# Four-layer graph network on one Trainium2 core: three steps of the next layer's projection change places beside the second attention

## The chip, the cores and the metric

The kernel runs on one core of one Trainium2 chip. The metric is the device time of one execution in microseconds. Three timed runs of the kernel before gave 2900.37, 2915.1 and 2917.88 us; the median is 2915.1. Beside them one execution was profiled, and it took 2553.76 us itself.

## The reference

There are 3327 nodes with 512 features each and a sparse 0/1 adjacency matrix. Four layers follow each other, each with a residual and a normalization ahead of it:

```
h = relu(layernorm(x));  x = x + layer(h, adj)
layer 0, 2, 3 (graph attention, 8 heads of 64):
    Wh = h @ W                       per head
    e[i,j] = leaky_relu(f_dst[i] + f_src[j], 0.2), only where adj[i,j] > 0
    out[i] = softmax_j(e[i,j]) @ Wh  (then a batch norm and relu, or an elu)
layer 1 (sage): relu(concat(h @ Ws, mean_of_neighbours(h) @ Wn) @ Wc)
```

The part that matters here is the step from layer 2 to layer 3. Layer 3 needs, for every node, its projected row Wh and two score terms per head. They can be made for a block of 128 nodes as soon as layer 2 has finished that block.

## The kernel before, in words

The nodes are cut into 26 blocks of 128, and each block into two groups of 64. For every group a list of neighbours is built first; the lists are up to 22 chunks of 128 neighbours long at the beginning and get shorter to 5 and 4 chunks at the end (`CAPS`). The attention, `attend`, walks over all groups in order. Its inner loop runs over units of at most three chunks:

- GpSimd (POOL) gathers the rows of the unit's neighbours out of a table in DRAM (L1165). A row holds 8 x 65 values scaled by exp(score) and 8 further factors.
- VectorE (DVE) takes the maximum of the row's factors and of the group's own factors R (L1266, `mx`), and multiplies by the mask (L1273, `wgt`). R comes from a small DRAM array, is loaded as `r_two`, and is spread over all partitions by a matmul (L1198, `r_bc`).
- TensorE multiplies weights and rows into `facc` (L1287).

Within the attention the order of instructions on TensorE, VectorE and ScalarE (ACT) is the order in which the Python code issues them, and every engine works its instructions off in that order. After each unit's two VectorE instructions, and before its matmuls, the loop calls `later()`. This advances each group that is being finished by one step (`sums`, `rd`, the eight scalings `fhp`, then `fin_e` and `fin_x`, which write the block of x), and then calls `tick()` of the next layer's projection.

That projection is the class `Following`. A finished block first goes through the normalization (`norm`, L777, in three steps: `ln_j`, `rs_h` and its companions, `ln_h`). Then a generator, `rest` (L841), does the block in steps that end at a `yield`. A tick advances the oldest block by one step, or by two where a second block is waiting; when a block ends, the next one begins in the same step:

```
for _ in range(min(2, len(self.ready))):
    while self.ready and next(self.ready[0]) is None:
        self.ready.pop(0)
```

The steps of `rest` before are: transposes into `p_ps` and relus into `hT` (L845, L848); scores `p_sd`, two exps into the row, and the copy `s_col` (L853 to L860); the clamp of `s_col` on VectorE and the matmuls `p_wh` (L863, L866); the two ACT instructions of `halves` that make `r_full` and `r_half` (L730, L731), the eight scalings `v_row` (L870) and the store of the table's rows; the subtraction that makes the lower half of R on VectorE (L734) and the transpose `p_tr` (L874); the copy `r_row` and its store to DRAM (L877 to L882). The PSUM tiles `p_ps`, `p_sd`, `p_wh` and `p_tr` of this layer share one buffer. Layer 2's own projection, beside layer 1, uses `rest_by_rows`, and layer 0's uses `Projection`; both call `halves` too.

When the last unit of layer 2 is done, `proj.drain()` runs the remaining ticks, and the last layer's attention begins.

Of the kernel before, what the change touches and what calls it, by code (L numbers as in the profile page):

```python
# [32 lines left out]
ALU = mybir.AluOpType  # L33
# [28 lines left out]
SMALL = 53.0  # L62
# [662 lines left out]
def halves(nc, pool, cs, sf):  # L725


    rf = pool.tile([P, H], F32, name="r_full", tag="r_full", bufs=2)
    rs = pool.tile([P, 2, H], F32, name="r_half", tag="r_half", bufs=2)
    nc.scalar.activation(rf, sf, AF.Exp, scale=0.8, bias=cs["down"])  # L730
    nc.scalar.copy(rs.bitcast(F32R)[:, 0, :], rf)  # L731

    def other():
        nc.vector.tensor_tensor(rs.bitcast(F32R)[:, 1, :], rf, rs[:, 0, :], ALU.subtract)  # L734
        return rs.rearrange("p t h -> p (t h)")

    return other


class Following:  # L740
# [100 lines left out]
    def rest(self, c, hx):  # L841
        nc, pp, WA, wl = self.tc.nc, self.pool, self.WA, self.wl
        tp = self.psum.tile([P, KC, P], F32, name="p_ps", tag="p_ps", bufs=self.pb)
        for kc in range(KC):
            nc.tensor.transpose(tp[:, kc, :], hx[:, kc * P : (kc + 1) * P], self.cs["ident"])  # L845
        hT = pp.tile([P, KC, P], F32, name="hT", tag="hT", bufs=2)
        for kc in range(KC):
            nc.scalar.activation(hT[:, kc, :], tp[:, kc, :], AF.Relu, accum_out=self.hs[:, c, kc : kc + 1])  # L848
        yield True
        self.mean(c, hT)  # L850
        sd = self.psum.tile([P, BANK], F32, name="p_sd", tag="p_ps", bufs=self.pb)
        for kc in range(KC):
            nc.tensor.matmul(sd[:, : 2 * H], hT[:, kc, :], WA[wl][:, kc, :], start=(kc == 0), stop=(kc == KC - 1))  # L853
        row = pp.tile([P, ROW], F32, name="v_row", tag="v_row", bufs=2)
        V = row[:, : H * (F + 1)].rearrange("p (h f) -> p h f", f=F + 1)
        d = sd[:, H : 2 * H]
        nc.scalar.activation(V[:, :, F : F + 1], d.rearrange("p (h o) -> p h o", o=1), AF.Exp)
        nc.scalar.activation(row[:, H * (F + 1) :], d, AF.Exp, scale=-0.8, bias=self.cs["down"])
        sf = pp.tile([P, H], F32, name="s_col", tag="s_col", bufs=2)
        nc.scalar.copy(sf, sd[:, :H])  # L860
        yield True

        nc.vector.tensor_scalar(sf, sf, -SMALL, SMALL, ALU.max, ALU.min)  # L863
        wh = self.psum.tile([P, D], F32, name="p_wh", tag="p_ps", bufs=self.pb)
        for kc in range(KC):
            nc.tensor.matmul(wh, hT[:, kc, :], self.Wt[:, kc, :], start=(kc == 0), stop=(kc == KC - 1))  # L866
        yield True
        rs = halves(nc, pp, self.cs, sf)
        for h in range(H):
            nc.scalar.mul(V[:, h, 0:F], wh[:, h * F : (h + 1) * F], V[:, h, F : F + 1])  # L870
        nc.sync.dma_start(self.table[c * P : (c + 1) * P, :ROW], row.bitcast(I32))
        yield True
        tr = self.psum.tile([2 * H, P], F32, name="p_tr", tag="p_ps", bufs=self.pb)
        nc.tensor.transpose(tr, rs(), self.cs["ident"])  # L874
        yield True
        rr = pp.tile([2 * H, P], F32, name="r_row", tag="r_row", bufs=2)
        nc.scalar.copy(rr, tr)  # L877
        n = P // GB
        nc.sync.dma_start(
            self.r_dram[c * n : (c + 1) * n, :, :, :].rearrange("g t h i -> (t h) g i"),  # L880
            rr.rearrange("h (g i) -> h g i", i=GB),
        )  # L882
        yield None
# [739 lines left out]
```

## Time and profile before

| | us |
|---|---|
| timed runs, median (lowest to highest) | 2915.1 (2900.37 to 2917.88) |
| profiled execution, its own time | 2553.76 |
| its span from the first to the last instruction | 2551.8 |
| DVE busy in the span | 1852.3 (73%) |
| PE busy in the span | 1825.0 (72%) |
| POOL busy in the span | 1387.4 (54%) |
| ACT busy in the span | 1068.3 (42%) |

The timed runs are 361 us longer than the profiled execution. The trace is of the profiled execution alone, so every duration below is compared with its 2553.76 us.

Lines such as "L870 ACT v_row" name the line of the kernel, the engine and the tile that is written. In timelines the first number is the start in microseconds from the beginning of the span, the second is the duration, and what stands in square brackets is the idle time of the engine just before and what ended it. "x8" counts instructions; a matmul of 32-bit numbers stands as two. In lists of waits the numbers are the total, the count and the longest, in microseconds. The stage of the change, in which layer 2's attention and layer 3's projection run side by side, lies between about 1500 and 2046 us of the span.

### The profile page before, as it was taken

The numbers are of one execution on the slowest core, as the hardware profiler recorded it, in microseconds if no ns is written. First come the engines' busy times: TensorE is split into PE (matmuls) and PEld (weight loads), VectorE is DVE, ScalarE is ACT, GpSimd is POOL, SyncE is SP. The second block draws the span as 40 slices with busy tenths as digits, with TensorE's granted clock in tenths as the row PEclk, the third lists the DMA queues.
The fourth block names the chain that finished last, engine by engine and source line by source line (L and its number), as shares of the span: only waits on it lengthen the run. The fifth ranks groups of instructions, "written<-read, shape, count | busy, mean of one in ns | idle before, by whom it ended". The sixth has DMA issues, their size and how long they took to land.

```text
span 2551.8 us, 53690 instructions
## 1 busy us (share of the span) xinstructions
PE 1825.0 (72%) x21112; PEld 1161.8 (46%) x21112; DVE 1852.3 (73%) x2272; ACT 1068.3 (42%) x3810; POOL 1387.4 (54%) x1482
## 2 busy tenths in 40 slices
PE   3667756776677698889999657778878646566653
PEld 2444444454454342223333356656555435555543
DVE  7667579999997850222333499999877279999996
ACT  4553212333445332334455214667766601233444
POOL 1000176777772026777777277776554067777672
PEclk9767889988888899999999778897877787777787
DMA  8773198888783566788888478887665178888784
GB/s 326 288 263 123 43 296 276 280 281 260 241 253 95 191 217 198 234 247 260 254 267 255 125 223 242 235 240 232 199 200 177 39 215 232 236 238 243 232 238 123
DMA packets 189057, 562.57 MB, mean 220 GB/s; under 512 B 37764, under 2 KB 42304, under 8 KB 185470
## 3 DMA queue, kind: packets, MB, share of 16 engines
q0 software_dynamic: 115456, 404.86, 53.3%
q1 hardware_dynamic: 73342, 154.20, 17.0%
q8 instruction: 169, 2.77, 0.4%
q14 instruction: 90, 0.74, 0.1%
HBM read 499.26 MB, written 59.68 MB: 219 GB/s over the span
## 4 chain that ended last, share of the span: by engine, by line
PE 30%; DVE 24%; issue 13%; ACT 9%; DMA 8%; POOL 3%; DVEq 0%; SPq 0%; POOLq 0%; ACTq 0%
DVE mx L1266 12%; PE facc L1287 8%; DVE wgt L1273 8%; PE sage_acc L1522 4%; DMA z_rows<-h_dram,idx 4%; PE p_wh L866 4%; DMA rows<-table,idx 3%; PE n_ps L1471 3%; PE p_wh L808 3%; ACT fhp L1225 2%; POOL z_rows L1165 2%; PE s_ps L1445 2%; POOL rows L1165 1%; ACT bn_y L1225 1%; ACT v_row L870 1%
## 5 line engine op out<-in xcount | busy, mean ns | idle before, releaser
L1165 POOL DMA_INDIRECT rows<-table,idx x1077 | 1027.7, 954 | 580.0 <-issue 224.5
L1287 PE MATMUL facc<-rows,wgt 128*64 128x65 f32 x17232 | 722.5, 253 | 393.7 <-DVE wgt L1273 259.7
L1287 PEld LDWEIGHTS facc<-rows,wgt 128*64 128x64 f32 x17232 | 667.1, 165 | 518.2 <-DVE wgt L1273 310.5
L1266 DVE TENSOR_TENSOR mx<-r_bc,rows 128x1536 f32<-128x1536 f32 (+1 forms) x405 | 639.4, 1579 | 48.4 <-DMA fin_x<-fx 17.7
L1273 DVE TENSOR_TENSOR wgt<-mx,mask 128x1536 f32<-128x1536 f32 (+1 forms) x405 | 638.4, 1576 | 42.3 <-DVE mx L1266 1.0
L1165 POOL DMA_INDIRECT z_rows<-h_dram,idx x359 | 340.7, 949 | 273.7 <-ACT hT L1442 141.0
L1225 ACT ACTIVATE fhp<-sums,rd 64x64 f32<-64x64 f32 x832 | 219.9, 334 | 305.4 <-DVE rd L1219 302.0
L1522 PE MATMUL sage_acc<-z_rows,z_mask 128*64 128x512 f32 x718 | 209.8, 618 | 33.0 <-DMA z_rows<-h_dram,idx 32.6
L1258 ACT ACTIVATE mask<-on 128x192 uint8<-128x192 uint16 (+1 forms) x135 | 46.5, 345 | 325.3 <-DVE on L1252 321.8
L1086 POOL DMA_DIRECT2D list_b<-shift x12 | 6.0, 503 | 271.7 <-DVE shift L1040 271.5
L811 DVE TENSOR_TENSOR sd_pr<-p_wh,ab 128x1024 f32<-128x1024 f32 x26 | 31.8, 1225 | 141.4 <-PE p_wh L808 141.4
L1522 PEld LDWEIGHTS sage_acc<-z_rows,z_mask 128*64 128x64 f32 x718 | 52.2, 137 | 156.2 <-issue 77.6
L680 PE MATMUL wh_ps<-fWt,hT 128*128 128x512 f32 x208 | 123.3, 748 | 0.0
L866 PE MATMUL p_wh<-fWt,hT 128*128 128x512 f32 x208 | 117.2, 714 | 1.4 <-ACT s_col L860 1.4
L1225 ACT ACTIVATE bn_y<-sums,rd 64x64 f32<-64x64 f32 x416 | 109.5, 333 | 2.4 <-DVE rd L1219 0.5
L1503 ACT CAST z_mask<-mask 128x128 f32<-128x128 uint8 (+1 forms) x196 | 52.7, 284 | 118.7 <-PE sage_acc L1522 117.5
L1476 DVE TENSOR_TENSOR s_o<-n_ps,bn_y 128x512 f32<-128x512 f32 x26 | 17.9, 690 | 116.2 <-PE n_ps L1471 116.2
L1215 ACT COPY sums<-facc 128x260 f32<-128x260 f32 x156 | 56.6, 363 | 104.7 <-DMA rows<-table,idx 77.7
L1471 PE MATMUL n_ps<-fWx,aT 128*128 128x512 f32 x208 | 98.7, 608 | 0.0
L808 PE MATMUL p_wh<-fWt,hT 128*128 128x512 f32 x208 | 96.9, 610 | 2.0 <-DVE hT L699 1.9
L1445 PE MATMUL s_ps<-fWx,hT 128*128 128x512 f32 x208 | 93.5, 603 | 3.4 <-ACT hT L1442 3.4
L1198 PE MATMUL r_bc<-r_two,fones 2*128 2x512 f32 x156 | 89.1, 575 | 6.6 <-DMA r_two<-r_dram 3.6
(213 smaller groups left out, 2146.3 us busy)
## 6 DMA issues: line engine op xcount, KB each, us to landing
adj_i<-in_adj SPq DMA_DIRECT2D x26, 1664.0 KB
table<-v_row SPq DMA_DIRECT2D x78, 264.0 KB
rows<-table,idx POOLq DMA_INDIRECT x1077
fin_x<-fx SPq DMA_DIRECT2D x52, 256.0 KB
ln_x<-in_x SPq DMA_DIRECT2D x26, 256.0 KB
bn_x<-in_x SPq DMA_DIRECT2D x13, 512.0 KB
fx<-bn_x SPq DMA_DIRECT2D x13, 512.0 KB
fsage_x<-fx SPq DMA_DIRECT2D x26, 256.0 KB
```

The costliest lines, as they stand in the source:

```text
L680: nc.tensor.matmul(wh, hT[:, kc, :], self.Wt[:, kc, :], start=(kc == 0), stop=(kc == KC - 1))
L808: nc.tensor.matmul(wh, hT[:, kc, :], self.Wt[:, kc, :], start=(kc == 0), stop=(kc == KC - 1))
L866: nc.tensor.matmul(wh, hT[:, kc, :], self.Wt[:, kc, :], start=(kc == 0), stop=(kc == KC - 1))
L1165: nc.gpsimd.indirect_dma_start(out=dst, out_offset=None, in_=src[:, :], in_offset=bass.IndirectOffsetOnAxis(ap=idx[:, k : k + 1], axis=0))
L1198: nc.tensor.matmul(rb, ones[0:2, :].bitcast(F32R), rrs.pop(g).bitcast(F32R), start=True, stop=True)
L1225: nc.scalar.mul(hp[o0 : o0 + GB, h * F : (h + 1) * F], sm[mine, q, 0:F], rd[mine, q, :])
L1266: nc.vector.tensor_tensor(mx[:, :n], rbs[g].unsqueeze(1).to_broadcast(full), gt[:, :n, H * (F + 1) : ROW].unsqueeze(3).to_broadcast(full), ...
L1273: nc.vector.tensor_tensor(wt[:, :n], mx[:, :n], mk.unsqueeze(2).to_broadcast(full), ALU.mult)
L1287: nc.tensor.matmul(accs[g][v * GB : (v + 1) * GB, q * (F + 1) : (q + 1) * (F + 1)], wt[:, k, h, :], gt[:, k, h * (F + 1) : (h + 1) * (F + 1)],
L1445: nc.tensor.matmul(ps, hT[:, kc, :], Wx[:, 0, kc, :], start=(kc == 0), stop=(kc == KC - 1))
L1471: nc.tensor.matmul(ps, aT[:, kc, :], Wx[:, 1, kc, :], start=(kc == 0), stop=(kc == KC - 1))
L1522: nc.tensor.matmul(acc[u * GB : (u + 1) * GB, :], m, z, start=f, stop=l)
```

## The change

The change moves instructions between the steps of `rest`. The clamp of `s_col` goes from the step of the `p_wh` matmuls to the step of the scalings. `halves` is issued behind the eight scalings and the table's store instead of ahead of the scalings. The subtraction for R's lower half stays a step of its own, and the transpose `p_tr` goes into the last step, together with the copy `r_row` and its store. No instruction is added or removed.

```
         nc.scalar.copy(sf, sd[:, :H])
         yield True
-
-        nc.vector.tensor_scalar(sf, sf, -SMALL, SMALL, ALU.max, ALU.min)
         wh = self.psum.tile([P, D], F32, name="p_wh", tag="p_ps", bufs=self.pb)
         for kc in range(KC):
             nc.tensor.matmul(wh, hT[:, kc, :], self.Wt[:, kc, :], start=(kc == 0), stop=(kc == KC - 1))
         yield True
-        rs = halves(nc, pp, self.cs, sf)
+
+        nc.vector.tensor_scalar(sf, sf, -SMALL, SMALL, ALU.max, ALU.min)
         for h in range(H):
             nc.scalar.mul(V[:, h, 0:F], wh[:, h * F : (h + 1) * F], V[:, h, F : F + 1])
         nc.sync.dma_start(self.table[c * P : (c + 1) * P, :ROW], row.bitcast(I32))
+        rs = halves(nc, pp, self.cs, sf)
+        yield True
+        rs = rs()
         yield True
         tr = self.psum.tile([2 * H, P], F32, name="p_tr", tag="p_ps", bufs=self.pb)
-        nc.tensor.transpose(tr, rs(), self.cs["ident"])
-        yield True
+        nc.tensor.transpose(tr, rs, self.cs["ident"])
         rr = pp.tile([2 * H, P], F32, name="r_row", tag="r_row", bufs=2)
         nc.scalar.copy(rr, tr)
```

More of the change, by code (lines that the diff above doesn't have):

```diff
@@ L861, in rest @@
         yield True
-        nc.vector.tensor_scalar(sf, sf, -SMALL, SMALL, ALU.max, ALU.min)
         wh = self.psum.tile([P, D], F32, name="p_wh", tag="p_ps", bufs=self.pb)
@@ L867, in rest @@
         yield True
-        rs = halves(nc, pp, self.cs, sf)
+        nc.vector.tensor_scalar(sf, sf, -SMALL, SMALL, ALU.max, ALU.min)
         for h in range(H):
@@ L871, in rest @@
         nc.sync.dma_start(self.table[c * P : (c + 1) * P, :ROW], row.bitcast(I32))
+        rs = halves(nc, pp, self.cs, sf)
+        yield True
+        rs = rs()
         yield True
         tr = self.psum.tile([2 * H, P], F32, name="p_tr", tag="p_ps", bufs=self.pb)
-        nc.tensor.transpose(tr, rs(), self.cs["ident"])
-        yield True
+        nc.tensor.transpose(tr, rs, self.cs["ident"])
         rr = pp.tile([2 * H, P], F32, name="r_row", tag="r_row", bufs=2)
```

## The prediction

> **What bounds the kernel now.** The change touches one generator, `rest`, which prepares the last layer's table while the attention of layer 2 runs. I first placed that stage in the trace (the first and last starts of the p_wh matmuls, L866: 1542.5 to 2041.2 us), then read the chain of waits inside it, then the timelines of TensorE, ScalarE (ACT) and VectorE (DVE) side by side, then the waits of DVE alone. I call the six pieces between the yields A (transpose, relu), B (scores p_sd, exps, s_col), C (p_wh), D (eight scalings v_row, table store), E (r_half on DVE, transpose p_tr) and F (r_row copy and store).
>
> From 1725 to 2012 us the chain is the same ring for every block of 128 rows:
>
> ```profile
> 1863.02 1.74 ACT v_row L870 x8
> 1864.76 0.03 issue
> 1864.78 1.06 ACT fhp L1225 x4
> ...
> 1869.62 0.15 ACT r_row L877
> 1869.77 0.04 issue
> 1869.82 1.13 PE p_ps L845 x4
> ...
> 1872.16 1.89 PE p_sd L853 x8
> 1874.05 0.72 PE r_bc L1198
> 1874.78 2.80 PE facc L1287 x48
> 1877.57 4.86 PE p_wh L866 x8
> 1882.44 0.02 issue
> 1882.46 1.74 ACT v_row L870 x8
> ```
>
> The reader is to see that no DVE line is in it. From the v_row scalings ACT works without a gap to r_row (1863.02 to 1869.77, 6.75 us); TensorE waits for r_row because all of `rest`'s PSUM tiles share one buffer, and then goes from p_ps to the end of p_wh (12.6 us). One turn is one block.
>
> The waits between 1725 and 2003 us, first DVE's longest, then TensorE's:
>
> ```profile
> DVE s_col L863 <- ACT s_col L860: 22.8, 11, 2.5
> DVE mx L1266 <- PE r_bc L1198: 11.5, 11, 1.8
> ...
> PE p_ps L845 <- ACT r_row L877: 39.2, 17, 4.3
> ```
>
> DVE does stand still in front of the clamp (22.8 us in 11 waits here; 31.6 in 14 over the stage, the other 8.8 in the drain after 2003). But DVE is early: its product for the 48 matmuls at 1874.78 was finished at 1868.1. So that stall is slack, while the wait for r_row is in the ring.
>
> Where the two ACT instructions of `halves` (r_full, r_half) sit today:
>
> ```profile
> 1860.64 0.28 ACT L730 ACTIVATE r_full<-s_col,fdown 128x8 f32<-128x8 f32 x1
> 1860.96 0.20 ACT L731 CAST r_half<-r_full 128x8 fp32r<-128x8 f32 x1
> 1863.02 1.74 ACT L870 ACTIVATE v_row<-p_wh,v_row 128x64 f32<-128x64 f32 x8 [1.86 <-PE p_wh L866]
> ```
>
> They end at 1861.16, and ACT then idles 1.86 us for p_wh: they are free.
>
> Ahead of 1725 us the lists are long and DVE is the bound, almost without gaps; after 2003 only the drain is left, a pure PE and ACT chain whose end starts the next layer's gathers:
>
> ```profile
> 1725.00:1808.00 83.00, 71.50 (x979) 52.53 (x981) 77.81 (x85) 59.63 (x236) 53.28 (x56) 0.83 0.76 226
> 1808.00:2003.00 195.00, 153.76 (x1931) 111.90 (x1927) 142.82 (x175) 137.26 (x536) 86.96 (x91) 0.78 0.56 171
> 2003.00:2046.00 43.00, 25.32 (x59) 13.34 (x59) 4.48 (x19) 23.11 (x101) 0.00 (x0) 0.72 0.08 32
> ```
>
> (Columns: PE, PEld, DVE, ACT and POOL busy us, granted clock, DMA share, GB/s.) DVE has 52 us to spare in the middle line.
>
> [...] eight p_sd passes take 1.06 or 1.89 us, 48 facc passes 1.62 or 2.87. [...] r_full over 8 columns measures 0.28 to 0.30 us.
>
> **The change, part by part.** I count six yields before and after, so the number of ticks, and which ticks a block shares with the next one (F, A and B in one tick, then C, D, E), stay as they are.
>
> 1. *Clamp from C to D* (26 DVE instructions of 0.17 us). Its s_col is now a tick old. The 22.8 us of stall go. What is late next: DVE reaches E's r_half earlier, and that now needs part 2. In the ring I gain nothing.
>
> 2. *`halves` from ahead of the scalings to behind them* (26 times r_full and r_half). In ACT's queue they now stand between v_row and the next layer work (fhp, sums, ln_s, ln_h, fin_e, fin_x, r_row). Cover gone: cost 0.32 us start to start plus 0.20, [...] I take 0.45 us per turn. The clamp they wait for is long done. Behind them waits r_row, and behind that TensorE's p_ps: the ring grows by 0.45.
>
> 3. *DVE's r_half* keeps its place in DVE's order, but its input comes after v_row. In the ring: v_row + 1.74 + 0.52, about 2.3 us after v_row starts, where DVE arrives some 2 us before. Behind it stands the next mx, which waits for r_bc until 1.5 to 2 us after the same start, so it is late by under 1 us against a lead of 6. Cost nothing in the ring. In the first block it does cost: r_half ran at 1547.84,
>
> ```profile
> 1547.84 0.18 DVE L734 TENSOR_TENSOR r_half<-r_full,r_half 128x8 fp32r<-128x8 f32 x1
> ```
>
> while v_row ran from 1547.72 to 1549.47. There DVE is the bound and will stand until 1550.0: +2.2 us. The later early blocks have room (v_row plus halves end at 1673.8, r_half at 1674.64).
>
> 4. *p_tr from E to F's tick*, one tick later on TensorE, with r_row at its old place on ACT. In the ring TensorE reaches it at about 4.2 us after v_row's start, r_row is at 6.6: hidden. Its old waits (21.4 us on TensorE) are in places where TensorE then waits for DVE anyway: no gain.
>
> 5. *Queues.* POOL's order is unchanged. On SP r_dram's store falls behind an r_two load in the first blocks only; later the order is the same. The stores slip with r_row.
>
> The sum:
> - first block, 2.2;
> - early blocks in which ACT's ln_j follows v_row directly and DVE waits for it (1651, 1671, 1691): 3 x 0.4 = 1.2; in the others the idle of 0.3 to 0.5 before ln_j hides it;
> - ring. The turns from v_row at 1807.90 to 2011.61 are 11, and alternate 18.05 and 19.49, together 37.54 = 11 windows of 3.413: the ring is locked to the clock's windows. With 0.9 more per pair that lock breaks; the next one is three turns in 17 windows, 19.34 each, or 0.57 more than today's 18.77: 11 x 0.57 = 6.3. The four turns from 1738.80 to 1807.90 (18.18, then 16.97) get 0.45 and an estimated 0.2 of slower clock: 2.6;
> - drain: the last two blocks have v_row, then p_tr within 0.04 us. Now r_full, r_half and DVE's r_half stand between: 0.52 + 0.17 + hand-overs of 0.06 = 0.75, twice, 1.5.
>
> Together 13.8, say +14 us. The profiled execution (2553.8 us, span 2551.8) becomes 2568, +0.55%. The timed runs are 14% longer than it (median 2915.1), for no reason that the profile shows; adding 14 gives 2929, scaling gives 2931. I take **2930 us**; own range 2917 to 2943, from no clock effect and half the ring cost to double the clock effect.
>
> **Rivals.**
> - *Clock tips over, slower.* The gap on TensorE ahead of p_sd (4.85 us from the last facc to p_sd at 1872.16) grows to 5.5 and each turn takes six windows of 3.413, 20.48. For: the lock seen. Against: the four turns at 16.97 drift freely. 11 x 1.71 + 4 x 20.48 - 69.1 + 4.9 = 36: 2915 + 36 to 41, about 2954.
> - *DVE paces after all, faster.* If in the timed runs TensorE and ACT have slack, the clamp stall of 22.8 us is real time: 2915 - 23 = 2892. It decides once DVE's own turn (mx and wgt 12.0, fin_x 1.4, the small ones 1.3, so 14.7 us of work, plus its stalls) is longer than the ring. For: DVE is busy 94% from 1725 to 1808. Against: no DVE in the chain after 1725, and r_half hands most of the stall back.
> - *Nothing to see.* The windows stay locked at 18.77 and swallow the 0.45; the first block and the drain remain, +4 to 6: 2920.
> - *The step count differs from the words* (seven): a seventh tick would lengthen the drain; the yields say six, so I leave it out.
>
> **How the numbers follow.** Forecast 0.60, clock 0.15, DVE 0.12, nothing 0.13. The range 2895 to 2958 holds most of the first and last and reaches to the two others. One per cent, about what a measurement of this kernel can tell from no change, is 29 us. Faster by more: half of DVE's share, 0.07. Slower by more: the clock's 0.15 and the upper tail of the forecast, 0.10, so 0.25. Within: 0.68.
>
> **What would show it.** Right: s_col at D without a wait; v_row followed by r_full and r_half at once; about 2 us of DVE wait at r_half per block, released by ACT's r_half; ring turns of 19.2 to 19.5; the first r_half at about 1550; p_tr 0.75 us later in the last two blocks. Wrong: turns of 18.77 or less with DVE in the chain (the DVE rival), or of 20.5 (the clock).

## The result and the profile after

| | before, us | after, us | ratio, 95% interval |
|---|---|---|---|
| measurement of the change | 2911.7 (2900.0 to 2921.5) | 2916.4 (2908.5 to 2929.2) | 1.0026 [1.0011, 1.0040] |
| the same, measured again | 2952.1 (2938.4 to 2974.1) | 2964.3 (2946.7 to 2975.5) | 1.0037 [1.0021, 1.0052] |
| the same, a third time | 2961.6 (2944.7 to 2981.3) | 2964.8 (2953.6 to 2976.2) | 1.0008 [0.9989, 1.0028] |

The medians differ by 4.7, 12.3 and 3.3 us, the last not distinguishable from nothing; the forecast was +14. The profiled execution of after took 2910.5 us (span 2908.7).

The kernel before took 2557 us in one measurement and 2907 to 2962 us in all others, one chip showed both, and the profiled execution of before (2553.8 us) is of the first kind; below they are called the short and the long condition.

Two readings of the trace of before that the forecast rests on, with their numbers. The window of 3.413 us: the granted clock in that trace is 1.00 or 0.50, and each of its 196 stretches but the last, with which the trace ends, lasts a whole number of times 3.413 us, 41 of them just once; in the trace of after the same holds of 264. At 1.00 the 48 matmuls of facc take 1.62 us (at 1864.42), at 0.50 2.87 (at 1874.70). In the ring of before the stretches from 1842.44 us on last 10.24 us at 1.00, 6.83 at 0.50, 10.24 at 1.00 and 10.24 at 0.50, and so three times more, up to 1992.63: 11 windows each time, 37.55 us, as long as two turns. The order of issue: TensorE stands idle for 2.49 us ahead of p_ps at 1869.82 and for 1.23 us ahead of p_sd at 1872.16, while the product for the matmuls behind them is finished at 1868.09; they start at 1874.70. ScalarE stands idle for 1.86 us ahead of v_row at 1863.02, while the rd for the fhp behind it is finished at 1860.04; fhp starts at 1864.78. On VectorE it is the trace of after that shows it: r_half waits 1.57 us and starts at 2062.86, and the mx behind it, whose r_bc ended at 2062.14, starts at 2063.06.

The chain of waits of after, through the 10th block (start, duration, what):

```profile
1992.01 1.75 ACT v_row L869 x8
1993.76 0.20 ACT r_full L730
...
1993.98 0.20 ACT r_half L731
...
1994.20 1.06 ACT fhp L1226 x4
...
1998.42 0.61 ACT fin_x L1317
1999.03 3.96 another core or an unknown queue
...
2003.01 0.26 ACT r_row L878
```

`halves` stands where the prediction put it, right behind v_row and ahead of fhp. New is the line of 3.96 us: ScalarE has nothing left but r_row and waits for a signal. The waits of after from 2039 to 2245 us, ten turns of the ring, from the 12th to the 22nd block (total, count, longest):

```profile
PE p_ps L845 <- issue: 19.3, 6, 3.9
...
ACT r_row L878 <- remote: 14.0, 10, 2.7
...
DVE r_half L734 <- ACT r_full L730: 11.7, 7, 2.0
```

VectorE's wait has moved from the clamp to r_half, as predicted; part 2 alone, below, has that wait too and costs nothing that can be measured. But TensorE now waits for "issue", that is for nothing the profile shows, and r_row for a "remote" signal, although the record of p_tr has ended. Neither stood in the ring of the profile before. Over the whole span the same word leads TensorE's waits. First the profile of before, then that of after:

```profile
PE facc L1287 <- DVE wgt L1273: 259.7, 177, 14.3
PE facc L1287 <- issue: 97.6, 47, 3.4
```

```profile
PE facc L1288 <- issue: 389.7, 757, 14.1
```

In the short condition TensorE mostly waits for VectorE's products, in the long one 757 times for nothing visible, in the middle of runs of matmuls.

### The profile page after: what moved, and what is told of

Same layout as the page of the kernel before. It is cut to its first block, busy times and chain, and to the rows that moved or that the text cites. A ratio compares the mean times of both kernels' runs of the same rounds, so it can differ in the third digit from the quotient of the medians.

```text
span 2908.7 us, 53721 instructions
## 1 busy us (share of the span) xinstructions
PE 2095.9 (72%) x21112; PEld 1334.8 (46%) x21112; DVE 1857.5 (64%) x2272; ACT 1073.1 (37%) x3810; POOL 1386.9 (48%) x1482
## 4 chain that ended last, share of the span: by engine, by line
PE 55%; issue 18%; ACT 6%; DVE 4%; DMA 2%; another core or an unknown queue 2%; POOL 1%; DVEq 0%; ACTq 0%; POOLq 0%; SPq 0%
PE facc L1288 29%; PE sage_acc L1523 5%; PE p_wh L864 4%; PE p_wh L808 3%; PE n_ps L1472 3%; PE r_bc L1199 3%; PE s_ps L1446 2%; PE fwx_ps L1365 1%; PE p_sd L853 1%; PE bmean_ps L1375 1%; DMA rows<-table,idx 1%; DVE mx L1267 1%; ACT fhp L1226 1%; ACT v_row L869 1%
## 5 line engine op out<-in xcount | busy, mean ns | idle before, releaser
L1288 PE MATMUL facc<-rows,wgt 128*64 128x65 f32 x17232 | 968.5, 266 | 426.7 <-issue 389.7
L1288 PEld LDWEIGHTS facc<-rows,wgt 128*64 128x64 f32 x17232 | 821.4, 175 | 645.8 <-issue 568.8
L1523 PE MATMUL sage_acc<-z_rows,z_mask 128*64 128x512 f32 x718 | 199.2, 620 | 8.5 <-DMA z_rows<-h_dram,idx 7.4
```

Source lines behind the costliest of these rows:

```text
L1288: nc.tensor.matmul(accs[g][v * GB : (v + 1) * GB, q * (F + 1) : (q + 1) * (F + 1)], wt[:, k, h, :], gt[:, k, h * (F + 1) : (h + 1) * (F + 1)],
L1523: nc.tensor.matmul(acc[u * GB : (u + 1) * GB, :], m, z, start=f, stop=l)
```

## The experiments

Every kernel was timed beside the kernel before on its own chip. Two stretches are read from each trace by the starts of v_row: four turns (9th to 13th block, the lists still 6 chunks long) and eleven turns (13th to 24th block). In the short profile of before they took 69.1 and 203.7 us. Each stretch is read from one profiled execution. few_gathers and few_2 were timed once, few_tr and few_after twice; the 169 to 216 us that the last three take off stand far outside the spread of before, the 14 us of few_gathers lie only 4 us below it (2547.7 to 2560.4).

| kernel | condition | ratio, 95% interval | four turns, us | eleven turns, us |
|---|---|---|---|---|
| before_again | long | 1.0005 [0.9990, 1.0019] | 88.1 | 220.3 |
| clamp_only, clamp_2 | long | 1.0010 [0.9995, 1.0025], 1.0004 [0.9990, 1.0018] | 88.0, 87.0 | 220.2, 217.0 |
| halves_only, halves_2 | long | 1.0005 [0.9989, 1.0021], 1.0005 [0.9989, 1.0021] | 84.2, 84.6 | 219.7, 220.3 |
| tr_only, tr_2, tr_3 | long | 1.0017 [1.0002, 1.0033], 1.0045 [1.0029, 1.0060], 1.0026 [1.0011, 1.0041] | 90.8, 92.3, 91.6 | 220.3, 227.0, 227.1 |
| after, after_again, after_3 | long | 1.0026, 1.0037, 1.0008 (above) | 92.5, 92.2, 92.6 | 220.7, 225.7, 223.8 |
| clamp_halves | short | 1.0046 [1.0029, 1.0063] | 73.2 | 210.1 |
| act_pad | short | 1.0160 [1.0141, 1.0179] | 80.8 | 224.2 |
| pe_pad | short | 1.0105 [1.0085, 1.0124] | 74.8 | 217.0 |
| act_pad_2 | long | 1.0051 [1.0032, 1.0071] | 87.0 | 227.3 |
| few_gathers | short | 2543.3 us beside 2557.3 | 70.6 | 203.9 |
| few_2 | long | 2745.1 us beside 2961.6 | 70.6 | 203.9 |
| few_tr | long | 2718.7 us beside 2907.2 | 69.5 | 205.6 |
| few_after | long | 2737.9 us beside 2907.2 | 71.5 | 210.1 |

**The parts one by one.** First the kernel before, unchanged.

> The kernel before, unchanged, profiled once more. If the profile of before that the prediction rests on stands for the timed runs, its span is near 2552 us again and a ring turn takes 18.1 or 19.5 us. If the timed runs are another regime (the profiled execution of the changed kernel took 2910 us, with TensorE standing still 390 us for nothing that the profile names), the span is near 2905 us, a ring turn takes about 20.5 us before the change too, and the clamp's wait on VectorE differs from 31.6 us. Ratio to before: 1.000.

It ran in the long condition and gave no difference, and "issue" ahead of facc stood at 367.0 us, so the pauses of TensorE are not the change's. Then part 1 alone:

```
-        nc.vector.tensor_scalar(sf, sf, -SMALL, SMALL, ALU.max, ALU.min)
         wh = self.psum.tile(...)
...
+        nc.vector.tensor_scalar(sf, sf, -SMALL, SMALL, ALU.max, ALU.min)
         rs = halves(nc, pp, self.cs, sf)
```

> Only the clamp goes one step later; halves stays ahead of the scalings and now needs the clamp of the same tick, and p_tr stays where it was. Theory (the ring of ScalarE and TensorE sets the time, halves behind the scalings costs 0.45 us a turn): the stall of VectorE at the clamp goes and nothing is gained, ratio 0.999 to 1.001. Rival (VectorE paces): 20 us or more faster, ratio 0.993.

> Part 1 alone: the clamp goes to the step of the scalings. Theory A (its stall is slack) ratio 0.999 to 1.001 in either condition. Rival B (the stall of 22.8 us in front of the clamp is real time): 0.991 to 0.996 at about 2555 us. Rival C (the clamp now delays r_full ahead of the scalings): 1.002 to 1.004.

No difference twice: the stall in front of the clamp was slack. Part 2 alone:

```
-        rs = halves(nc, pp, self.cs, sf)
         for h in range(H): ...
         nc.sync.dma_start(self.table[...], ...)
+        rs = halves(nc, pp, self.cs, sf)
```

> Only r_full and r_half go behind the scalings. Theory: this part carries the whole cost, +7 to +14 us, ratio 1.0025 to 1.005. Rival (the cost comes from p_tr, late on TensorE): ratio 1.000.

> Part 2 alone: `halves` behind the scalings, clamp and p_tr where they were. If the kernel before takes about 2555 us: theory A (ring) +10 to +14 us, ratio 1.004 to 1.0055, late turns with a mean of 19.2 to 19.4; rival B (the clamp's move is needed for the cost, since it lets DVE run into r_half) ratio below 1.002. If it takes about 2915 us, as in the first job with this edit: 0.999 to 1.002 again.

No difference twice, where the forecast had its whole ring cost. Where the room comes from can be read in the traces. In nine of the eleven turns of before_again, hT starts 1.6 to 1.7 us behind the end of the p_ps record, which releases it; in halves_only it is 0.8 to 1.2 us. `halves` makes p_ps later, and a delay that was there already becomes shorter by as much. Part 4 alone:

```
-        nc.tensor.transpose(tr, rs(), self.cs["ident"])
-        yield True
+        rs = rs()
+        yield True
+        tr = self.psum.tile(...)
+        nc.tensor.transpose(tr, rs, self.cs["ident"])
```

> Only p_tr goes into the last step, with r_row. Theory: TensorE has it done before ScalarE comes to r_row, ratio 0.999 to 1.001. Rival (ScalarE now waits at r_row for TensorE, which runs late in the timed runs): +5 us or more, ratio 1.002 or above.

> Part 4 alone: p_tr goes into the last step. If the kernel before takes about 2555 us: theory A (hidden in the ring, as predicted) ratio 0.999 to 1.001, late turns 18.05 and 19.49; rival B (r_row and p_ps wait for the later p_tr in every turn) ratio 1.002 or more. At about 2915 us: 1.0017 again, with the pause of about 3 us between p_tr and r_row in place of between p_ps and hT.

> Part 4 alone. Theory A (its cost needs TensorE to run late, behind its records, as at 2916 to 2952 us): at 2557 us 0.999 to 1.0015, late turns 18.05 and 19.49; at 2916 to 2952 us 1.0015 to 1.005. Rival B (a fixed cost of the hand-over r_row, p_ps): 1.002 to 1.005 in both.

Slower three times, by 0.17 to 0.45%. As far as the intervals tell, part 4 carries the whole cost in the long condition: parts 1 and 2 alone are each within 0.25% of nothing, and the two together were not met there. The table shows where: the four turns take 84 to 88 us without part 4 and 91 to 93 us with it, in every kernel. The eleven turns are longer in tr_2 and tr_3, but not in tr_only.

The two timelines of TensorE say how. The kernel before, in the long condition (before_again):

```profile
2002.77 1.47 PE L1287 MATMUL facc<-rows,wgt 128*64 128x65 f32 x42 [0.50 <-issue]
2004.17 0.66 PE L845 MATMUL p_ps<-fident,ln_h 128*128 128x128 f32 x4
2008.94 1.89 PE L853 MATMUL p_sd<-WA,hT 128*128 128x16 f32 x8 [4.12 <-ACT hT L848]
```

and ScalarE's next to it:

```profile
2003.26 0.24 ACT L877 COPY r_row<-p_tr 16x128 f32<-16x128 f32 x1
2007.75 0.28 ACT L848 ACTIVATE hT<-p_ps 128x128 f32<-128x128 f32 x1 [4.26 <-remote]
```

r_row is early, p_ps follows the matmuls at once, and its record ends at 2004.83; yet ScalarE gets the signal for hT only at 2007.75, 2.92 us later. After the change:

```profile
1998.07 1.53 PE L1288 MATMUL facc<-rows,wgt 128*64 128x65 f32 x44 [1.10 <-issue]
1999.53 0.28 PE L876 MATMUL p_tr<-fident,r_half 128*16 128x128 f32 x1
2003.32 1.12 PE L845 MATMUL p_ps<-fident,ln_h 128*128 128x128 f32 x4 [3.51 <-ACT r_row L878]
2005.67 1.89 PE L853 MATMUL p_sd<-WA,hT 128*128 128x16 f32 x8 [1.23 <-ACT hT L848]
```

Now p_tr stands behind those matmuls. Its record ends at 1999.81, r_row starts at 2003.01: the same late signal, 3.20 us, has moved from p_ps to p_tr. What used to be over by then comes behind it: r_row, the hand-over, and p_ps, until hT at 2004.47, 1.46 us. The other turns are alike: in the four turns hT of before_again starts 1.6 to 2.9 us behind the end of the p_ps record, and r_row of after 2.1 to 3.3 us behind that of p_tr. From the start of the last matmuls to p_sd it is 6.17 us before and 7.60 after. Four such turns are 5.7 us; the four turns are 4.4 us longer (92.5 against 88.1).

That TensorE was still at work in those 2.92 and 3.20 us, behind the ends of its records, is the author's estimate; no run shows what it did then.

**The change without part 4.** Against the kernel after:

```
-        rs = rs()
-        yield True
         tr = self.psum.tile(...)
-        nc.tensor.transpose(tr, rs, self.cs["ident"])
+        nc.tensor.transpose(tr, rs(), self.cs["ident"])
+        yield True
```

> The change without part 4: the clamp and `halves` move, p_tr stays in the step of r_half. Theory A (the cost of the change sits in p_tr's move into the last step, where r_row and then p_ps wait for a late TensorE): no measurable difference, ratio 0.999 to 1.001, and the turns of blocks 8 to 12 as before (three longest after the early blocks 23.1, 21.5, 22.8 us, not 23.8, 23.6, 23.8, 21.3). Rival B (halves behind the scalings lengthens the ring, as predicted): 1.0015 to 1.003 and ring turns up to 0.45 us longer.

This measurement met the short condition, and both sides missed: two parts that each cost nothing at 2916 us cost 0.46% here, 11.8 us, and the eleven turns went from 203.7 to 210.1 us. Some groups of three turns come near the lock that was forecast: 18.32, 19.62 and 19.92 us make 57.87, and 17 windows of 3.413 are 58.02. The mean of the turns stays below it, as the part on the prediction shows.

**More work for one engine.** Ten copies on ScalarE, or a first quarter of p_wh done twice on TensorE:

```
         nc.sync.dma_start(self.table[...], ...)
+        pd = pp.tile(...)
+        for _ in range(10):
+            nc.scalar.copy(pd, sf)
```

```
+        nc.tensor.matmul(wh, hT[:, 0, :], self.Wt[:, 0, :], start=True, stop=True)
         for kc in range(KC): ...
```

> The kernel before with ten small ACT copies (128x8) behind the scalings of every block, about 1.1 us of ACT time per block between v_row and r_row, more than twice what `halves` adds there. Theory A (in these runs TensorE's own rate sets the turn and ACT's string has slack): at most +4 us, late turns stay near 20.5. Rival B (the ring of the prediction, through ACT): 15 turns times 1.1, +16 us or more, ratio 1.0055. Rival C (turns locked to six clock windows, 20.48): either nothing or a jump to seven windows, 23.9, in some of the 11 turns, +20 to +38 us.

> The kernel before with the first quarter of the p_wh matmuls done twice, about 1.1 us of TensorE time per block. Theory A (TensorE's rate sets the turn): 1.1 us times 22 to 26 blocks, +24 to +29 us, ratio 1.008 to 1.010. Rival B (ring through both engines): 15 turns times 1.1, about +16 us, and the early blocks, bound by VectorE, hide the rest. Rival C (clock windows): nothing, or +20 to +38 us by jumps to seven windows.

> Ten small ACT copies behind the scalings again, 1.1 us a block; at 2557 us they cost 1.6%, with turns of exactly 20.48 us. Theory A (at 2916 to 2952 us the turns stand at six clock windows already, 20.5 us, and ACT's string has slack within them): ratio 0.999 to 1.003. Rival B (ScalarE is in the ring there too): 1.005 or more, turns of 21.5. At 2557 us: 1.016 again.

The copies turned out twice as long as expected, the 1.1 us having been the author's estimate; in the trace of act_pad they push fhp from the end of v_row to 1903.09 us:

```profile
1899.17 1.75 ACT L870 ACTIVATE v_row<-p_wh,v_row 128x64 f32<-128x64 f32 x8 [1.79 <-PE p_wh L866]
1900.76 2.31 ACT L874 COPY pad<-s_col 128x8 f32<-128x8 f32 x10
1903.09 2.14 ACT L1228 ACTIVATE fhp<-sums,rd 64x64 f32<-64x64 f32 x8
```

so some 2.2 us a block and not 1.1. In the short condition that cost 38 us, and the late turns are 20.48 us each, six windows of the clock: the ring passes ScalarE's time on (15 turns of 2.2 would be 33), and the turn comes out at whole windows; rival C had the six windows, but its jump to seven did not come. TensorE's extra matmuls cost 25 us, which is theory A's sum and not rival B's 16: 1.2 us in each of the eleven turns, where both theories have 1.1, and the rest in the early blocks, the four turns and the drain. That TensorE's time counts everywhere does not take ScalarE out of the ring, which act_pad shows in it. In the long condition the same 2.2 us cost 0.51%, about 15 us, less than half: neither side is right as it stood. ScalarE's string has room there for the 0.45 us of `halves`, but not for 2.2: in most of the eleven turns of act_pad_2 hT starts 0.04 us behind the p_ps record, so the delay is used up. Of these 15 us only 3.2 have a place, behind the 24th block (v_row to the last r_row, 35.5 against 32.3 us in halves_2 and clamp_2); the rest is not separated from the run-to-run spread of the stage.

**Fewer gathers.** In layers 2 and 3 only the first chunk of a unit is gathered, and it serves the unit's other chunks:

```
-                for k in range(n):
+                for k in range(n if layer == 0 else 1):
                     gather(gi[:, k, :], table, k0 + k)
...
```

Two more lines, left out here, make VectorE and TensorE read that chunk; their instructions keep their number.

> The kernel before, where in layers 2 and 3 only the first chunk of each unit is gathered and serves all its chunks, so about 60% of the gathered bytes of these two attentions are left out; VectorE's and TensorE's instructions keep their number and shapes. Theory A (the pauses of TensorE that stand as issue come with the DMA load of the gathers): the issue idle ahead of facc falls from 367 us to under 200 and the two attentions run as in the profiled execution of before, some 200 us shorter. Rival B (the pauses have nothing to do with the gathers): issue idle stays above 300 us and the time within 40 us of before.

> Only the first chunk of each unit is gathered in layers 2 and 3 and serves all its chunks; at 2557 us this changed the time by -14 us. Theory A (at 2916 to 2952 us TensorE's issue pauses come with the DMA load of the gathers): issue idle ahead of facc in these layers falls by more than half and the time by 100 to 200 us. Rival B (pauses independent of the gathers): time within 40 us of before.

The first of the two met the short condition, where nothing much was to be gained (-14 us). In the long condition the same edit takes off 216 us, and TensorE's waits over the span of few_2 read

```profile
PE facc L1287 <- issue: 220.9, 288, 3.4
PE facc L1287 <- DVE wgt L1273: 139.1, 104, 14.0
```

against 382.8 us in 744 waits in act_pad_2 on the same chip; what is left above the 93.8 us of few_gathers lies ahead of layer 2, where all gathers remain. From the first facc matmul of layer 2 to the end of the span few_gathers takes 1085.3 us and few_2 1085.2, where before takes 1093.8 and before_again 1273.5. So the pauses go away with the gathers, and with them the difference between the conditions in these layers. The edit also leaves out GpSimd's work of issuing the gathers; whether that or the transfers disturb TensorE was not parted. About 205 us of the ring by engine, first before_again (ten turns, 12th to 22nd block), then few_2 (eleven turns, 13th to 24th) (busy us of PE, PEld, DVE, ACT and POOL, granted clock, DMA share, GB/s):

```profile
2041.00:2246.00 205.00, 156.42 (x1864) 109.80 (x1864) 141.95 (x172) 130.31 (x510) 93.91 (x99) 0.78 0.60 173
```

```profile
2004.00:2208.00 204.00, 161.34 (x1947) 115.95 (x1947) 143.63 (x181) 143.44 (x562) 34.95 (x37) 0.77 0.31 92
```

The clock is nearly the same; in the same time few_2 gets through 1947 matmuls and 562 ScalarE instructions in place of 1864 and 510, with half the DMA share: one turn more. The ring itself is back: few_2's turns alternate 18.05 and 19.49 us, and the waits from 2004 to 2208 us show r_row and hT waited for as in the short profile:

```profile
PE p_ps L845 <- ACT r_row L877: 28.5, 11, 3.5
...
ACT hT L848 <- PE p_ps L845: 10.5, 11, 1.2
```

where before_again, from 2041 to 2246 us, has ten waits of 2.4 us for a late signal:

```profile
ACT hT L848 <- remote: 24.2, 10, 2.9
```

hT starts 0.04 us behind the p_ps record in every turn of few_2. So the change could be measured in the ring of the prediction, without the pauses.

> The whole change, where only the first chunk of each unit is gathered in layers 2 and 3 (two thirds of the gathers of a long unit left out), which takes TensorE's pauses out of the stage. Read in the trace: v_row from the 10th to the 23rd block takes 238.3 us without the change. Theory A (the ring of the prediction): 11 turns times 0.57 and some tenths in the four turns of 17, so 245 to 249 us, late turns with a mean of 19.2 to 19.5. Rival B (part 4 adds in every turn): above 251. Rival C (the ring takes no extra): 238 to 241.

> Part 4 alone on the same base with only the first chunk of each unit gathered in layers 2 and 3. Theory A (hidden in the ring, as predicted): 238.3 us again within 1 us, turns 18.05 and 19.49. Rival B (r_row and p_ps wait for the later p_tr): 242 us or more.

The whole change takes the stretch from the 10th to the 23rd block to 245.2 us, as theory A had it, the eleven turns from 203.9 to 210.1 us, and the stage, first facc matmul of layer 2 to the last r_row, from 582.1 to 592.4, +10.3 us. The chain of few_after:

```profile
2062.55 1.75 ACT v_row L869 x8
2064.30 0.20 ACT r_full L730
...
2064.51 0.20 ACT r_half L731
...
2069.57 0.15 ACT r_row L878
...
2069.77 1.03 PE p_ps L845 x4
```

From the start of v_row to that of p_ps it is 7.22 us, against 6.80 in the prediction's ring (1863.02 to 1869.82) and in few_2: 0.42 for `halves`. p_ps follows r_row at once; no pause. VectorE waits, harmlessly:

```profile
2064.74 0.17 DVE L734 TENSOR_TENSOR r_half<-r_full,r_half 128x8 fp32r<-128x8 f32 x1 [2.08 <-ACT r_half L731]
```

Part 4 alone keeps most turns at 18.05 and 19.49; the stretch from the 10th to the 23rd block took 239.6 us, 1.3 more than without it and so a little outside what theory A allowed. The eleven turns are 1.8 us longer, 1.4 of it in the last one (17.99 in place of 16.56); the drain has 1.0 us more, and the stage as a whole 3.5.

The whole change with all its gathers, twice more:

> The whole change again. In the job before this one the kernel before took 2557 us, as in its profiled execution, and the change without part 4 cost 0.46% (about 12 us), with late ring turns of 18.3 to 19.9 us in place of 18.05 and 19.49. Theory A (the ring of the prediction decides wherever the kernel before takes about 2555 us, and where it takes about 2915 us TensorE's own pauses swallow it): at 2555 us the whole change costs 0.4 to 0.7%, +10 to +18 us; at 2915 us 0.1 to 0.4%. Rival B (the measured +0.26% is the change's cost in both conditions): ratio 1.0026 again, +6 to +8 us. Theory C (part 4 adds to part 2): ratio above 1.006 at 2555 us.

> The whole change. Theory A: where the kernel before takes about 2557 us, 1.004 to 1.0065 (parts 1 and 2 cost 1.0046 there, part 4 nothing or a little on top); where it takes 2916 to 2952 us, 1.0025 to 1.0045 once more. Rival B: the same ratio, below 1.004, in both conditions.

Both met the long condition. What the whole change costs in the short condition with all gathers was not measured; clamp_halves is nearest to it.

## Why the prediction was wrong

- **The step that failed** is the last of the sum: "The timed runs are 14% longer than it (median 2915.1), for no reason that the profile shows; adding 14 gives 2929". The 14 us were worked out for the ring of the short execution and carried over to runs in the long condition. There the two terms that matter come out the other way: part 2, the 8.9 us of the ring (6.3 and 2.6), measures nothing, and part 4, put at nothing as "hidden", costs 0.17 to 0.45%.
- **Part 2**, 0.45 us a turn, the author's estimate a little under the 0.52 us of the two instructions (0.32 and 0.20). Right in its ring: 0.42 us measured on ScalarE, and ten of the eleven turns are 0.44 us longer in few_after. The surcharge for the clock is not there: those ten turns have a mean of 19.17 us, not the 19.34 of three turns in 17 windows. That the eleven together give +6.2 us (few_after) and +6.4 (clamp_halves) against the forecast 6.3 is luck, since 1.9 of it falls on the last turn. The prediction took all eleven turns for 18.77 us; the last one was 16.56 before. In the long condition it costs nothing that can be measured; in the traces it shortens a delay of some 1.6 us that TensorE's signal has anyway.
- **Part 4**, costed at nothing. In the ring few_tr keeps its turns, though the stage is 3.5 us longer. In the long condition it is the cost. The sentence "In the ring TensorE reaches it at about 4.2 us after v_row's start, r_row is at 6.6: hidden" assumes that a p_tr that has been issued is also finished; there its signal comes 2.1 to 3.3 us behind its record in the four turns, in the middle of the one place where ScalarE and TensorE wait for each other.
- **Part 1 and part 3**: no gain and no ring cost, as said. The first block's 2.2 us did not come. In after VectorE does wait 3.2 us for the first r_half, but the turn behind that block's v_row is 39.98 us in place of 39.89 in before_again; in few_2 r_half runs 4.5 us behind v_row without the change, so that base has no such wait to show.
- **The other terms**, on few_after against few_2: everything ahead of the 9th block +1.9 (3.4 forecast for the first and the early blocks), the four turns +0.8 (2.6), the drain from the 24th block's v_row +1.4 (1.5). The stage is +10.3 against 13.8.
- **A reading that was off**: p_ps waiting 39.2 us for r_row is the sum over the whole stage; from 1725 to 2003 us, the stretch that the prediction names, it is 34.5 us in 15 waits. The ring stands without it.
- **The rivals.** DVE's is out: both clamp runs show no difference. "Nothing to see" was nearest in size (+4 to 6), but not for its reason: the turns were not locked at 18.77. The clock's six windows exist, but in the long condition they are there before the change: from the 13th to the 22nd block nine turns of before_again take 184.3 us, 54.0 windows of 3.413, and those of tr_only take 184.3 and those of after 184.1. In the trace of after the granted clock keeps the same beat: from 2057.23 to 2241.55 us it is 1.00 and 0.50 in turn, 10.24 us each. That such a lock swallowed the 0.45 us was not shown; whether it or TensorE's late signals set the turn there, these runs do not part. In the later measurements the same nine turns take 187.5 us in after_again, 55 windows, and 190.9 in tr_2, 56, where clamp_2 and halves_2 beside them take 183.4. There part 4's cost in the late turns looks like whole windows.

That a profile 346 us shorter than the shortest timed run is hardly of the same kind was to be seen beforehand. The right forecast from it would have kept the sum as one case, and a stage bound by something unseen, with the cost of each part open, as the other.

## What to carry to other kernels

Where the profiled execution and the timed runs differ by more than the runs' own spread, take the profile's critical ring as one of two cases, and get a second profile before pricing instructions in it. In these traces the signal of a TensorE instruction came up to 3.3 us behind the end of its record: before putting one last ahead of a hand-over to another engine, look for waits put down to "remote" or "issue" there. Here a transpose issued a step ahead of its reader was worth 0.17 to 0.45% in the long condition.

## What was not expected of the hardware

- The same kernel on the same chip took 2557 us in one measurement and 2916 us in another. The difference shows as pauses of TensorE in the middle of runs of matmuls, mostly of 0.2 to 1.1 us (97.6 us in 47 waits in the short profile, 367.0 in 750 in the long one of the same kernel). The busy time of the same 17232 facc matmuls grows too, from 722.5 to 977.1 us (968.5 in after): of the intervals between their starts 627 lie between 0.5 and 0.8 us (634 in after), where the short profile has 22. With fewer gathers in layers 2 and 3 the difference vanishes from those layers. Why TensorE's pauses come with the gathers in one condition and not in the other is open. The bytes moved are the same, and so are the 169 and 90 packets of the two instruction queues, too few for a pause each.
- Some turns came out at whole windows of the granted clock, which are 3.413 us long in the traces of before and after. Turns of 20.48 us, one after the other, in act_pad and act_pad_2 are six of these, and the pair of 18.05 and 19.49 us in before is eleven. There work did not cost its length: in act_pad ten copies of 2.2 us cost 1.9 us a turn (224.2 against 203.7 us over eleven turns). What makes the clock change, and what ties the turns to it, was not shown.
- Small ScalarE instructions in a row did not overlap in act_pad: the ten copies of 128x8 took 2.31 us, 0.23 us each from start to start, where one lasts 0.20. All ten write the same tile, and copies to different tiles were not run.
